# Three pieces of work moved inside the first units of a four-layer graph network: scaled values, the table of empty rows, and the softplus of two constants

## The chip, the cores and the metric

The kernel runs on one core of a Trainium2 chip. A core has a matrix engine (TensorE, PE in the profile; its weight loads are PEld), a vector engine (VectorE, DVE), an engine for activation functions (ScalarE, ACT), a general engine (GpSimd, POOL) and SyncE (SP), which here only issues DMA transfers. Each engine takes its own instructions strictly in the order of the program, and engines wait for each other through semaphores. The metric is the device time of one execution in microseconds; the kernel before took 1411.94 us, the median of three runs from 1405.89 to 1412.65.

## The reference

A batch of 8 graphs shares one adjacency matrix of 2048 x 2048 nodes; each node has 64 features. There are four layers, each with a residual and a layer norm around it. Layers 0, 1 and 2 are attention layers, layer 3 is a gated mean over neighbours. Cut to what matters:

```
# layer 0 (layers 1 and 2 alike, without the node weights and the inner norm)
h  = layernorm((x * node_weights + node_bias + x) @ W) * gamma + beta
s1, s2 = h @ a1, h @ a2
e  = leaky_relu(s1[:, :, None] + s2[:, None, :], 0.2)
att = softmax(where(adj > 0, e, -9e15), axis=-1)
x  = layernorm(x + elu(att @ h + h))
# layer 3
feat   = softplus(x * (w0 / sqrt(2)) + b0)
scores = feat * wa + ba
attn   = softmax over the neighbours j of scores[j, d], for each feature d
x  = layernorm(x + sum_j attn[i, j, d] * feat[j, d])
```

A row of the adjacency without any neighbour gets a softmax over equal numbers, which is the plain mean over all nodes. The kernel needs three small things for this: a table of the empty rows, the mean of the values, and, for layer 3, a bound on the scores, which it takes from the softplus of the two largest inputs that are possible.

## The kernel before, in words

A *unit* is one layer of one graph. Its 2048 x 2048 weights are made and used in 16 tiles of 128 neighbours by 2048 rows. For tile `jb` the vector engine makes `w` with one instruction (maximum of a row term and a per-neighbour term, times the mask: `weights`, line 981), and the matrix engine multiplies it in eight matmuls of 512 columns onto two PSUM banks `acc` (`products`, line 1030). The left operand of these matmuls is `pv`, the values scaled by an exponential of their score (`prepare`, line 811). There are four buffers for `w`, so VectorE can be up to four tiles ahead. The list `todo` orders the units: layer 0 of graphs 0 to 3, layer 1 of the same, layer 0 and 1 of graphs 4 to 7, and then layer 2 of all, with layer 3 beside and behind it. The first unit is number 0, the fourth is number 3, both in layer 0.

Everything else of a unit (its features, its scores, the norm behind it) is written as Python generators, which a `Streams` object (line 1358) steps once per tile. A generator yields where it wants to wait for a number of steps. All PE, DVE, ACT and POOL instructions are kept in the order in which the Python code issues them (`InOrder`, line 70), so this stepping decides what stands behind what in each engine's queue; no scheduler changes it later. What is waited for in one instruction holds everything behind it on the same engine.

The first unit is special in four ways.

- Its features are made by `features0(0)` (line 665) before any product. Its last part makes the normalised values `y` on ACT, completes them on POOL (`settle`), adds the 16 blocks of `y` in a *tree* of four POOL additions (8, 4, 2 and 1 blocks), and multiplies the sum by ones on PE (`p_mean`); then `mean_pieces` (line 613) splits the mean into three bf16 pieces, with ACT and DVE in turn. After the tree the loop that drives the start breaks off (`ready(0, 0)`), and `prepare(0, 0)` (line 1410) issues `pv` on POOL. In the queues the first tile's products are followed on PE by `p_mean`, and the fifth `w` on DVE stands behind the first piece of the mean.
- Its mask is still being made. `mask` (line 280) compares the adjacency rows with zero on DVE (`edge`, two instructions each) and counts neighbours on PE (`p_deg`, 16 tiny matmuls). Nine masks are made before the unit and seven during tiles 0 to 6, one ahead of each tile's `w`.
- After the last mask, `empties` (line 328) reads the counts on DVE (`empty`, `half_ldeg`), spreads them out (`em`), transposes them on PE (`p_empty`, four matmuls), and copies the result on DVE (`emptyT`). `emptyT` is read by the last matmuls of every unit; `half_ldeg` and `empty` are read only in layers 2 and 3.
- Its row term lies in SBUF; from unit 1 on the row term `r` is made by PE in PSUM ahead of the last products of the unit before (`spread`, line 827), with `Banks.use("psR", 1)` taking over the PSUM banks that `p_deg` and `p_empty` used.

`constants` (line 433) starts at tile 3 of the first unit. It makes the right operands `rh` of the three layers and the score operands, on POOL, PE and ACT, and then the bound for layer 3: `softplus` of `ext` (line 381: Abs, Exp, then Ln and Relu on ACT, then one addition `fext` on DVE), two products and a shift on POOL (`l3off`, `l3b`) with a maximum on DVE between them, and six small DVE instructions (`beyond`, `fext`). `beyond` is next used by `group(0)` before layer 2, `l3off` by layer 3. Ln lies in another table of activation functions than Exp, so ACT loads a table ahead of Ln and again ahead of the next Exp.

The features of the next units also run beside unit 0. `features0(1)` and `features0(2)` scale `x` on ACT (`xs`, one buffer), transpose it on PE (`p_xT`), copy it on ACT (`xT`) and multiply it on PE (`p_h`). Between `p_xT` and `xT` of graph 2, ACT's queue holds the 16 `xs` activations of graph 3 and eight `y` activations of graph 1.

Of the kernel before, what the change touches and what calls it, by code (L numbers as in the profile page):

```python
# [18 lines left out]
P = 128  # L19
# [31 lines left out]
def gnn4_kernel(ctx: ExitStack, tc: tile.TileContext, t, out):  # L51
# [326 lines left out]
    nc.gpsimd.memset(ext[:, 1:2], -X_MAX)  # L378
    fext = consts.tile([P, 2], F32, name="fext")

    def softplus(f, y, src):

        act.activation(y, src, AF.Abs, scale=l3c[:, 0:1], bias=l3c[:, 1:2])
        act.activation(y, y, AF.Exp, scale=-1.0)
        yield 1
        act.activation(y, y, AF.Ln, bias=1.0)
        act.activation(f, src, AF.Relu, scale=l3c[:, 0:1], bias=l3c[:, 1:2])
        yield 1
        dve.tensor_tensor(f, f, y, ALU.add)

    rs_w, last_w, a_cols = [], [], [None]
# [41 lines left out]
    def constants():  # L433

        for layer in range(3):
            rs, last = rs_w[layer], last_w[layer]
            rr = early.tile([P, F1], F32, tag="rr", name=f"rr_{layer}", bufs=2)
            pool.memset(rr, 0.0)
            pool.tensor_tensor(rr[:, :F], rs[:, :F], last, ALU.subtract)
            if layer == 0:  # L440
                pool.tensor_tensor(rr[:, :F], rr[:, :F], gamma, ALU.mult)
                for h in range(2):
                    pool.tensor_scalar(
                        rr[h * F : h * F + 1, :F], beta[h * F : h * F + 1], 2.0, None, ALU.mult
                    )
            for h in range(2):
                pool.memset(rr[h * F : h * F + 1, F:], 1.0)
            rh = consts.tile([P, 2, F1], F32, name=f"rh_{layer}")
            pool.memset(rh, 0.0)
            yield 1  # L450
            for h in range(2):
                sl = slice(h * F, (h + 1) * F)
                pool.tensor_copy(rh[sl, h, :], rr[sl])
            RH.append(rh)
            if layer == 0:
                AS.append(None)
                continue
            yield from pm_slots.take()
            p = psum(f"p_rt_{layer}")
            pe.transpose(p[:F, :P], rr[:, :F], ident)  # L460
            yield 1
            rt = early.tile([F, P], F32, tag="rt", name=f"rt_{layer}", bufs=1)
            act.copy(rt, p[:F, :P])
            pm_slots.give()
            yield from pm_slots.take()
            p = psum(f"p_as_{layer}")
            pe.matmul(p[:, :2], lhsT=rt, rhs=a_cols[layer], start=True, stop=True)
            as_ = consts.tile([P, 2, 2], F32, name=f"as_{layer}")
            pool.memset(as_, 0.0)
            yield 1  # L470
            for h in range(2):
                sl = slice(h * F, (h + 1) * F)
                act.copy(as_[sl, h, :], p[sl, :2])
            pm_slots.give()
            AS.append(as_)
        pool.tensor_tensor(ident2, ident[:, :F], ident[:, F:], ALU.add)
        pool.tensor_scalar(l3c[:, 0:1], l3c[:, 0:1], INV_SQRT2, None, ALU.mult)
        yield 1
        yield from softplus(fext, small.tile([P, 2], F32, tag="sp", name="sp_ext", bufs=1), ext)
        l3b = small.tile([P, F], F32, tag="l3b", name="l3b", bufs=1)  # L480
        pool.tensor_tensor(l3off, wa, fext[:, 0:1].to_broadcast([P, F]), ALU.mult)
        pool.tensor_tensor(l3b, wa, fext[:, 1:2].to_broadcast([P, F]), ALU.mult)
        dve.tensor_tensor(l3off, l3off, l3b, ALU.max)
        pool.tensor_scalar(l3off, l3off, -1.0, HEADROOM, ALU.mult, ALU.add)
        yield 1
        dve.tensor_reduce(beyond, wa, AX.X, ALU.max, apply_absolute_value=True)
        dve.tensor_tensor(fext[:, 0:1], fext[:, 0:1], fext[:, 1:2], ALU.subtract)
        dve.tensor_tensor(beyond, beyond, fext[:, 0:1], ALU.mult)
        dve.tensor_scalar(fext[:, 1:2], beyond, -1.0, None, ALU.mult)
        dve.tensor_tensor(beyond, beyond, fext[:, 1:2], ALU.max)  # L490
        dve.tensor_scalar(beyond, beyond, -L3_SPAN, None, ALU.add)
# [173 lines left out]
    def features0(b):  # L665

        n = f"0_{b}"
        step = K2 if b < NB else 4
        x = x_cur[b].v
        xs = early.tile([P, K, F], F32, tag="xs", name=f"xs_{b}", bufs=1)  # L670
        for k in range(K):
            act.activation(
                xs[:, k],
                x[:, k],
                AF.Identity,
                scale=nodes[:, k : k + 1],
                bias=nodes[:, K + k : K + k + 1],
            )
            if k % step == step - 1:
                yield 1  # L680
        yield from h_slots.take()
        yield from xT_slots.take()
        xT = tmp.tile([P, K2, P], F32, tag="xT", name=f"xT_{b}")
        sums = small.tile([P, 2], F32, tag="sums", name=f"sums_{b}", bufs=4)
        yield from transposed(xT, sums, xs, n)
        h = tmp.tile([P, K, F2], F32, tag="h", name=f"h_{b}")
        g0 = 0
        while g0 < 4:
            width = Banks.width()
            ps = []  # L690
            yield from pm_slots.take(width)
            for g in range(g0, min(g0 + width, 4)):
                p = psum(f"p_h_{b}_{g}")
                for k in range(2):
                    pe.matmul(
                        p[:, k * 2 * F2 : (k + 1) * 2 * F2],
                        lhsT=xT[:, 2 * g + k],
                        rhs=w0c.rearrange("p h f -> p (h f)"),
                        start=True,
                        stop=True,  # L700
                    )
                ps.append((g, p))
            yield 1
            for g, p in ps:
                act.copy(
                    h[:, 4 * g : 4 * g + 4, :], p[:, : 4 * F2].rearrange("p (k f) -> p k f", f=F2)
                )
            pm_slots.give(width)
            g0 += width
        xT_slots.give()  # L710
        yield from sq_slots.take()
        sq = tmp.tile([P, K, F], F32, tag="sq", name=f"sq_h_{b}")
        act.activation(sq, h[:, :, :F], AF.Square)
        yield 2
        st = small.tile([P, 2, K], F32, tag="st", name=f"st_h_{b}", bufs=4)
        if b < 2:
            dve.tensor_reduce(st[:, 1], sq, AX.X, ALU.add)
            sq_slots.give()
            yield from inv_std(st, K, f"h_{b}", centered=True)
        else:  # L720
            yield from side_stats(sq, f"h_{b}", st)
        rs = st[:, 1]
        sc = S[0, b] = Scores()
        s = small.tile([P, 2, K], F32, tag="s0", name=f"s_{n}")
        dve.tensor_tensor(
            s, h[:, :, F:].rearrange("p k w -> p w k"), bc_k(rs, 2, K), ALU.mult
        )
        dve.tensor_tensor(s, s, bc_f(s_off, 2, K), ALU.add)
        exponentials(sc, s[:, 0], s[:, 1], s, 0, b, n)()

        if in_psum(0, b):
            yield from pm_slots.take()
            p = psum(f"p_r_{n}")
            pe.transpose(p[:K, :P], sc.e[:, 0], ident)
            yield 1
            rows_term(sc, p[:K, :P], n, 0, b)
            pm_slots.give()
        else:
            first_row(sc)
        y = rows_tile(early, "y", f"y_{b}")  # L740
        for k in range(K):
            act.activation(y.block(k), h[:, k, :F], AF.Copy, scale=rs[:, k : k + 1])
            if k % step == step - 1 and k < K - 1:
                yield 1
        h_slots.give()
        y.settle()
        V[0, b] = y
        yield from e_slots.take()
        tree = tmp.tile([P, K2, F], F32, tag="e", name=f"tree_{b}")
        src = y.v  # L750
        for m in (8, 4, 2, 1):
            pool.tensor_tensor(tree[:, :m], src[:, :m], src[:, m : 2 * m], ALU.add)
            src = tree
        yield 3
        yield from pm_slots.take()
        p = psum(f"p_mean_{n}")
        pe.matmul(p[:, :F], lhsT=ones, rhs=tree[:, 0], start=True, stop=True)
        e_slots.give()
        yield 1
        yield from mean_pieces(sc, p[:, :F], n)  # L760
# [639 lines left out]
    for i, _ in enumerate(first):  # L1400
# [6 lines left out]
            bg.step()  # L1407
        if ready(0, 0):
            break
    prepare(0, 0)  # L1410
    prepared.add(0)
    for layer in range(3):
        load_constants(layer)
# [22 lines left out]
    for n, (layer, b) in enumerate(todo):  # L1436
# [10 lines left out]
        for jb in range(K):  # L1447
            if n == 0:
                while masks < min(K, 9 + jb):
                    mask(p_deg, masks)  # L1450
                    masks += 1
                    if masks == K:
                        empties(p_deg)
            now[2] = jb
            reach(K * n + jb)
            u = units[n]
# [540 lines left out]
```

## Time and profile before

| what | value |
|---|---|
| median of three runs | 1411.94 us |
| profiled execution | 1418.37 us, its span 1416.6 us |
| busy: PE, DVE, ACT, POOL | 87%, 85%, 58%, 54% of the span |
| chain that ended last | PE 51%, DVE 21%, ACT 12%, POOL 8% |
| first product of unit 0 | 60.02 us |
| first product of unit 1 | 125.25 us |
| PE busy in 90 to 120 us | 21.14 of 30 us |
| PE busy in 150 to 180 us | 28.61 of 30 us |
| mean granted clock of TensorE | 0.94 |

Nearly every instruction has line 80 in the profile (the helper that keeps the order), so instructions are told apart by the tile that they write. `acc` is a product, `w` a weight tile, `edge` a mask. One tile's products are eight matmuls; they take 1.87 to 1.94 us at full clock and 3.68 us at half clock. In a list in order of time, the brackets at the end of a line give the idle time of the engine ahead of it and what ended it.

### The profile page before, as it was taken

Reading aid. Unit: us, or ns where it says so; the run is one execution under the profiler, and the core shown is the slowest. Engines: PE = TensorE matmul, PEld = TensorE weight load, DVE = VectorE, ACT = ScalarE, POOL = GpSimd, SP = SyncE. Lnnn points to the kernel's source line nnn. Section 1 sums busy time; section 2 is a strip of 40 time slices with the busy share of each in tenths; the row PEclk is TensorE's granted clock in tenths of the full one; section 3 lists DMA queues with packets and bytes.
Section 4 is the critical chain, followed back from the end, with each engine's and each line's share of the span. In section 5 each row is a group of like instructions: output and inputs, shape, how many; then the busy total and the mean of one; then the engine's idle time right before and its main releaser. Section 6 shows DMA issues by size and latency. Waiting matters only on the chain.

```text
span 1416.6 us, 19533 instructions
## 1 busy us (share of the span) xinstructions
PE 1232.4 (87%) x7169; PEld 628.2 (44%) x7169; DVE 1208.4 (85%) x1108; ACT 821.6 (58%) x1593; POOL 758.5 (54%) x1075
## 2 busy tenths in 40 slices
PE   3587989899898997999999878789989899976996
PEld 3233323334343332343333323245654555666996
DVE  3777989999998999989999788998879798977876
ACT  3434544565666553556546997877576767664442
POOL 1435776556765674554553432534455565666665
PEclk9698989999999998999999897999999999998998
DMA  8640000000000121222101000025543434511111
GB/s 293 210 103 1 2 1 2 1 2 1 3 2 0 48 88 45 91 91 62 61 2 39 1 15 1 22 60 144 140 138 85 135 105 134 159 40 34 35 38 33
DMA packets 112010, 87.24 MB, mean 62 GB/s; under 512 B 57917, under 2 KB 90845, under 8 KB 110882
## 3 DMA queue, kind: packets, MB, share of 16 engines
q1 hardware_dynamic: 111538, 85.79, 20.8%
q8 instruction: 59, 0.97, 0.3%
q14 instruction: 45, 0.37, 0.1%
q10 hardware_dynamic: 368, 0.12, 0.0%
HBM read 60.40 MB, written 25.45 MB: 61 GB/s over the span
## 4 chain that ended last, share of the span: by engine, by line
PE 51%; DVE 21%; ACT 12%; POOL 8%; issue 6%; DMA 2%; SPq 0%; DVEq 0%; POOLq 0%; ACTq 0%
PE acc L80 28%; PE p_l L80 14%; DVE w L80 13%; ACT w L80 2%; PE p_o L80 2%; ACT x L80 2%; DVE o L80 2%; PE r L80 2%; PE p_s L80 2%; POOL sq_x L80 1%; POOL tree L80 1%; ACT y L80 1%; ACT xs L80 1%; POOL st_x L80 1%; DMA raw<-in_adjT_dram 1%
## 5 line engine op out<-in xcount | busy, mean ns | idle before, releaser
L80 DVE SCALAR_TENSOR_TENSOR w<-r,se,edge 128x2048 f32<-128x2048 f32 (+1 forms) x270 | 552.9, 2101 | 29.2 <-PE r L80 22.9
L80 PE MATMUL acc<-w,pv 128*64 128x512 f32 x2048 | 501.3, 624 | 59.7 <-DVE w L80 38.6
L80 DVE SCALAR_TENSOR_TENSOR w<-r,lo_g,edge 128x2048 f32<-128x2048 f32 (+1 forms) x144 | 297.8, 2097 | 26.8 <-PE acc L80 14.6
L80 ACT ACTIVATE w<-w,down_g 128x2048 f32<-128x2048 f32 (+1 forms) x144 | 256.9, 1809 | 64.4 <-DVE w L80 57.3
L80 PEld LDWEIGHTS p_l<-v,mask 128*128 128x128 f32 x2048 | 256.3, 196 | 61.8 <-issue 48.5
L80 PE MATMUL acc<-w,x 128*64 128x512 f32 x1024 | 265.2, 648 | 17.6 <-ACT w L80 14.9
L80 PE MATMUL p_l<-v,mask 128*128 128x256 f32 x2048 | 271.1, 291 | 10.6 <-POOL mask L80 7.0
L80 PEld LDWEIGHTS acc<-w,pv 128*64 128x64 f32 x2048 | 134.7, 140 | 318.1 <-issue 190.7
L80 POOL TENSOR_TENSOR sq_x<-sq_x 128x32 f32<-128x32 f32 (+4 forms) x207 | 110.1, 532 | 63.8 <-ACT sq_x L80 49.4
L80 PEld LDWEIGHTS acc<-w,x 128*64 128x64 f32 x1024 | 67.4, 144 | 139.3 <-issue 88.9
L80 ACT ACTIVATE x<-o,st_x 128x64 f32<-128x64 f32 x256 | 91.6, 445 | 12.2 <-POOL st_x L80 12.2
L80 ACT ACTIVATE nd<-p_l,empty 128x256 f32<-128x256 f32 x64 | 30.2, 471 | 109.3 <-PE p_l L80 109.3
L80 ACT ACTIVATE o<-p_o,den 128x64 f32<-128x64 f32 x256 | 55.8, 323 | 45.9 <-DVE den L80 45.9
L80 PE MATMUL p_o<-rh,oT 128*128 128x130 f32 x384 | 61.6, 297 | 23.4 <-DVE o L80 6.7
L80 ACT COPY oT<-acc 128x512 f32<-128x512 f32 x48 | 25.7, 587 | 89.4 <-PE acc L80 89.4
L80 PEld LDWEIGHTS p_o<-rh,oT 128*128 128x128 f32 x384 | 50.1, 197 | 57.7 <-issue 33.7
L80 POOL TENSOR_TENSOR st_x<-isw_x,mhalf 128x16 f32<-128x16 f32 x24 | 70.5, 2938 | 1.9
L80 POOL TENSOR_TENSOR eh<-eh,x 128x1024 f32<-128x1024 f32 (+2 forms) x24 | 36.4, 1530 | 44.8 <-ACT eh L80 44.8
L80 DVE RECIPROCAL nd<-nd 128x256 f32<-128x256 f32 x32 | 55.7, 1742 | 0.0
L80 POOL TENSOR_TENSOR d<-x,wa_bc 128x1024 f32<-128x1024 f32 x8 | 19.0, 2380 | 66.7 <-DVE x L80 66.7
L80 POOL CAST rT<-rT 16x128 bf16<-16x128 f32 x45 | 15.2, 339 | 66.4 <-ACT rT L80 62.9
L80 POOL TENSOR_TENSOR sq_x<-o 128x512 f32<-128x512 f32 x23 | 29.2, 1270 | 34.6 <-DVE o L80 34.1
(258 smaller groups left out, 1543.8 us busy)
## 6 DMA issues: line engine op xcount, KB each, us to landing
mask<-mask_d SPq DMA_DIRECT2D x132, 256.0 KB
mask_d<-mf SPq DMA_DIRECT2D x32, 512.0 KB
raw<-in_adjT_dram SPq DMA_DIRECT2D x8, 1024.0 KB
raw<-in_adjT_dram SPq DMA_DIRECT2D x16, 512.0 KB
x<-in_x_dram SPq DMA_DIRECT2D x8, 512.0 KB
x_d<-x SPq DMA_DIRECT2D x8, 512.0 KB
e<-x_d SPq DMA_DIRECT2D x64, 64.0 KB
out_dram<-o SPq DMA_DIRECT2D x64, 64.0 KB
```

The source lines that it names most:

```text
L80: ins = f(*args, **kwargs)
```

## The change

Three things move; no instruction is added or taken away on any engine, and SP's queue has the same order as before.

- `prepare(0, 0)` is called inside `features0(0)` ahead of the tree, so `pv` of unit 0 stands ahead of the four tree additions in POOL's queue.
- `empties` is issued at tile 13 of unit 0, where before it was issued behind the last mask, ahead of tile 7's `w`. On DVE its four instructions now stand behind the tile 12 `w` and ahead of the tile 13 `w`; on PE the four `p_empty` matmuls stand behind the products of tile 12.
- `constants` waits until unit 3 has begun before the softplus of `ext`, and this softplus leaves four steps, not one, between its Relu on ACT and its addition on DVE. In the queues: the ACT instructions now stand around the scores of layer 1, graph 0; the DVE addition `fext` and `l3off` behind tile 5's `w` of unit 3; the six small DVE instructions behind tile 6's `w`; the three POOL instructions behind the splitting of `rT`. ACT still loads tables twice for it, the second time ahead of the Exp of unit 2's `eh`.

```diff
-    def softplus(f, y, src):
+    def softplus(f, y, src, layer=2):
 
         act.activation(y, src, AF.Abs, scale=l3c[:, 0:1], bias=l3c[:, 1:2])
         act.activation(y, y, AF.Exp, scale=-1.0)
         yield 1
         act.activation(y, y, AF.Ln, bias=1.0)
         act.activation(f, src, AF.Relu, scale=l3c[:, 0:1], bias=l3c[:, 1:2])
-        yield 1
+        yield 1 if layer == 2 else 4
         dve.tensor_tensor(f, f, y, ALU.add)
...
         pool.tensor_scalar(l3c[:, 0:1], l3c[:, 0:1], INV_SQRT2, None, ALU.mult)
-        yield 1
-        yield from softplus(fext, small.tile([P, 2], F32, tag="sp", name="sp_ext", bufs=1), ext)
+        while now[1] < 3:
+            yield 1
+        yield from softplus(fext, small.tile([P, 2], F32, tag="sp", name="sp_ext", bufs=1), ext, 0)
         l3b = small.tile([P, F], F32, tag="l3b", name="l3b", bufs=1)
...
         y.settle()
         V[0, b] = y
+        if b == 0:
+            prepare(0, 0)
         yield from e_slots.take()
         tree = tmp.tile([P, K2, F], F32, tag="e", name=f"tree_{b}")
...
         if ready(0, 0):
             break
-    prepare(0, 0)
     prepared.add(0)
...
                 while masks < min(K, 9 + jb):
                     mask(p_deg, masks)
                     masks += 1
-                    if masks == K:
-                        empties(p_deg)
+                if jb == K - 3:
+                    empties(p_deg)
```

## The prediction

> **What bounds the kernel now.** I read the page's shares first, then the chain that ended last in order of time, then DVE, PE, POOL and ACT in order of time from 45 to 130 us. Over the whole span PE (87%) and DVE (85%) are both nearly full, so a change at the start is worth what it takes from the start: later units repeat the same queues and hand a shift on. The start is not full, and the chain shows why. From the chain, start and length in us:
>
> ```profile
> 47.49 4.27 POOL tree L80
> ...
> 56.03 3.95 POOL pv L80
> 60.02 3.68 PE acc L80 x8
> 63.71 0.62 PE p_mean L80 x2
> ...
> 110.29 1.28 ACT L80
> ```
>
> The reader sees three places that the change touches: `pv` behind the tree, PE starting when `pv` ends, and the table load ahead of Ln in the middle of unit 0. DVE in order of time gives the stalls with their releasers:
>
> ```profile
> 64.90 0.29 DVE L80 SCALAR_TENSOR_TENSOR mean<-mean,later,mean 128x64 f32<-128x64 bf16 x1 [6.68 <-ACT mean L80]
> 83.23 0.18 DVE L80 TENSOR_SCALAR empty<-p_deg 128x16 f32<-128x16 f32 x1 [3.56 <-PE p_deg L80]
> 84.61 0.69 DVE L80 CAST emptyT<-p_empty 128x512 bf16<-128x512 f32 x1 [0.75 <-PE p_empty L80]
> 85.22 6.87 DVE L80 SCALAR_TENSOR_TENSOR w<-row,se,edge 128x2048 f32<-128x2048 f32 x3
> 112.10 0.16 DVE L80 TENSOR_TENSOR fext<-fext,sp_ext 128x2 f32<-128x2 f32 x1 [10.20 <-ACT fext L80]
> 113.06 2.34 DVE L80 SCALAR_TENSOR_TENSOR w<-row,se,edge 128x2048 f32<-128x2048 f32 x1
> 115.64 2.19 DVE L80 TENSOR_TENSOR beyond<-beyond,fext 128x1 f32<-128x1 f32 x1
> ```
>
> PE in order of time shows what these cost it, and that it comes back slowly after a gap:
>
> ```profile
> 83.92 0.66 PE L80 MATMUL p_empty<-ident,em 128*128 128x128 f32 x4 [0.73 <-DVE em L80]
> 87.62 6.29 PE L80 MATMUL acc<-w,pv 128*64 128x512 f32 x16 [3.04 <-DVE w L80]
> 109.75 1.90 PE L80 MATMUL p_h<-w0c,xT 128*128 128x132 f32 x8 [5.04 <-ACT xT L80]
> 115.46 3.68 PE L80 MATMUL acc<-w,pv 128*64 128x512 f32 x8 [3.82 <-DVE w L80]
> 119.08 1.88 PE L80 MATMUL r<-row,ones 3*128 3x512 bf16 x4
> 120.89 3.30 PE L80 MATMUL acc<-w,pv 128*64 128x512 f32 x8
> ```
>
> One tile is 3.68 us at half clock and 1.94 at full clock. The stretches of 2 us show the granted clock at 1.00 in 84 to 86 us, 0.53 in 86 to 88, 0.50 to 92 and 0.76 in 92 to 94: the 3.04 us gap closed it, and it opened some 5.4 us after work came back (93.0 less 87.62). After 60.02 it took 9.5 us, after 115.46 8.2 us.
>
> **Part one, `pv` ahead of the tree.** POOL and DVE take turns here: `tree` of 512 columns takes 4.26 us at 47.49 but 1.26 at 106.37, where DVE is idle, and `pv` takes 3.94 here and 1.90 at 109.33. `pv` begun at 47.49 gets its turn when the DVE work of 47.08 to 50.5 is over, so it ends near 52.4 (49.3 to 50.5, plus 1.9). That frees PE 7.6 us earlier for one tile only: the next PE instruction is `p_mean`, and it now waits for the tree. What is late next is therefore the tree, not `pv`. POOL's five instructions are the same and their turns lie between the same DVE instructions, so I put the tree's end at 60.0, about where `pv` ended (59.97); bounds are 58.1, if all additions slip in between masks, as the third and fourth did, and 63.1, if POOL gets no turn until DVE's fourth `w` ends at 58.2 (1.9 + 2.8 + gaps). `p_mean` was at 63.63, so it comes 3.6 us earlier. DVE's stall of 6.68 shrinks by the same. Behind `p_mean`, PE needed 19.56 us up to the last count (83.19), with the clock opening 5.9 us in. PE now has a gap before `p_mean`, so it opens 5.4 to 9.5 us in; between nothing and 1.8 us are lost, I take 0.7. The last count ends at 60.0 + 19.56 + 0.7 = 80.3: part one is worth 2.9 us (from -1.3, with the tree at 63.1 and the full clock loss, to 5.5). The reloads of the adjacency issued by masks 12 and 13 shift along: they are released by DVE, and 2 MB landed between 57 and 64 us at 258 to 420 GB/s, so they stay hidden. The constants' small POOL instructions (60 to 64.5 us) lose DVE's idle time as cover. About ten of them may have to wait a turn; they have until `st_h` at 78.75, 14.23 us of idle POOL, so I cost them at nothing. No moved step issues a transfer, and SP's queue keeps its order.
>
> **Part two, the empty rows' table at tile 13, with part three's removal of the softplus from unit 0.** Call the end of the last count T (83.19 before, 80.3 after).
>
> - At tile 7 DVE no longer waits for the counts (3.56) and the transposes (0.75). It goes on from the last mask, which ended 3.5 us ahead of T, so tile 7's `w` is ready at T - 1.2, and PE goes on at full clock. Before, PE idled 0.73 + 3.04 us and then ran two tiles in 6.29 instead of 3.8.
> - Tiles 7 to 11 with `p_rt`, `p_r`, `p_as` and `p_xT` took 13.5 us (87.62 to 101.13), 11.0 at full clock. DVE's `w` at 2.3 us each with 0.6 for `s` reach tile 11 at T + 8.6, PE wants it at T + 8.2. So `p_xT` ends near T + 11.8. POOL's `st_h` (3.08 us, begun at 78.75) is no longer beside an idle DVE; if it holds tile 7's `w` back until its end that is 2.1 us, if not, nothing. DVE's masks ran at their usual 1.31 beside it, so I take nothing and keep 2.1 for the range.
> - Tile 12 ends at T + 13.7, `p_empty` (0.66) at T + 14.4, `emptyT` 0.7 later, then `w` of tile 13 (2.34): its products start at T + 17.4. The gap of 3.0 us is the same as at tile 7, and again closes the clock: 3.68, to T + 21.1.
> - The next PE work is `p_h`, which waits for ACT's `xT`. That took 8.6 us from the end of `p_xT` (101.13 to 109.75), of which 0.5 was the softplus' first two activations; so it is ready at T + 19.9. Before, this wait stood open as 5.04 us; now it lies under the gap and the slow tile. The moved bubble is thus mostly free.
> - `p_h` 1.9 at half clock to T + 23.0; tile 14's `w` has long been ready, as DVE's wait of 10.20 for `fext`, 0.66 for `l3b` and the 3.0 us of the six small instructions are gone. The clock opens 5.4 to 8.2 us after T + 17.4, so tile 14 takes 2.6 and `r` ends 1.0 later, at T + 26.6.
> - Before, `r` ended at 120.89 = T + 37.7. The two are worth 11.1 us at `r`, from 8.2 (`st_h` holds DVE and the clock stays shut) to 12.6. PE's own first product of unit 1 gains a little more, but unit 1 is paced by DVE, whose nine `w` from 141.29 on follow each other without a gap, and DVE starts behind `r`. POOL's `tree` and `pv` of unit 1 ran on an idle DVE (106.37 to 111.2); now they lie beside the last `w`. Even if they wait for DVE's last `w` at about T + 22, 5 us more end before the first product of unit 1 at T + 29.7.
>
> **Part three, what unit 3 pays.** On ACT, the Abs, Exp, table load, Ln and Relu fall into the idle stretch 214.0 to 216.3 us (ACT waits 2.32 us for `p_r` at 216.31), some 8 us ahead of DVE's addition at about 224, so DVE doesn't wait for ACT. DVE pays 0.16 + 0.66 + 0.22 us for `fext`, the wait for POOL and `l3off`, then 0.8 us for six instructions, and up to 2 us more if POOL's addition to `o` (2.38 at 226.09) blocks one of them as it did `mean` there (2.10 at 226.45); that block is paid already today. I take 2.0. This stretch is DVE's on the chain (`w` 219.62 to 237.65), so it counts in full. PE's wait of 1.67 us at 229.2 becomes about 3.2, at the border of closing the clock; closed, it costs up to 2.3 us more. I take half of it, in all 3.0 lost (bounds 1.0 and 5.0). The second table load, 1.28 us ahead of an Exp at 229.82, delays POOL's `eh` and `pv` of a unit that starts at 255, 20 us later: nothing.
>
> **Sum.** 2.9 + 11.1 - 3.0 = 11.0 us less. The profiled execution (1418.37, of which 1.8 lie outside its span) becomes 1407.4; it stands 6.4 above the median, so the median becomes 1400.9.
>
> **The rivals.**
>
> - *The clock stays open in the moved gap.* It needs the 3.0 us gap at tile 13 and the 3.2 us one in unit 3 to end before the gate falls; 84 to 88 us speaks against it, the open clock behind the 1.67 us gap at 230.87 a little for it. Tile 13 then takes 1.94 and ends at T + 19.3, `p_h` begins at T + 19.9 and takes 1.1, tile 14 and `r` end at T + 23.9: 2.7 more, and 1.0 in unit 3, in all 14.7 less, 1397.2. The Trainium skill's "TensorE: Matmul & The Clock Gate", section "What's actually happening", states this: the gate goes by free-running windows of about 3.4 us, so a shorter gap need not close it. By that rule both outcomes are open from one run to the next; the trace's 3.04 us gap closed it.
> - *Part one does nothing, because `p_mean` takes over from `pv`.* If the tree ends at 63.1, 11.1 - 3.0 = 8.1 less or a little under, 1403.8. For it speaks that PE's order has `p_mean` second; against it that the third and fourth addition slipped in between masks.
> - *Half of the gain is lost on the way:* `st_h` holds DVE, the clock stays shut long in units 0 and 3, the tree is late. 0.5 + 8.2 - 5.0 = 3.7 less, 1408.2, no measurable change.
> - *The stall moves along (slower).* If ACT gives `fext` in unit 3 as late as in unit 0, DVE waits 10.20 us there, with a shut clock afterwards (1.75 for each of two tiles) and 3.0 for the rest: 16.7 lost against 14.0 won, 1414.6. It decides from a wait of about 7.5 us, that is with `fext` later than 231 us on the old axis. Against it: the four steps left, and ACT's queue, which is empty at 214.
>
> **How the numbers follow.** The forecast has 0.50, the open clock 0.08, part one at nothing 0.12, half the gain 0.18, the moved stall 0.07, and 0.05 stays for shifts in later units that I can't see. Half a per cent, 7.1 us, is about what a measurement can tell from no change. Faster takes the first two and most of the third, 0.68; same the rest of the third, the fourth and half of the fifth, 0.24; slower 0.08. The range leaves out the far end of the open clock and the moved stall: 1395 to 1410. The likeliest case alone is 1397 to 1405.
>
> **What would show it.** In the new profile: `pv` on POOL ends by 53 and one tile's products stand alone on PE, followed by a gap that `p_mean` ends at about 60; no DVE wait at tile 7, and tile 7's products without a gap ahead of them; a gap of about 3 us on PE ahead of tile 13, with half clock behind it; no wait of DVE for ACT's `fext` anywhere; unit 1's first product at 109 to 111 us instead of 125.25; in unit 3 DVE about 2 us later at tile 7. The forecast is wrong if the first product of unit 1 comes after 116, if DVE waits for `fext` in unit 3, or if the lead at unit 1 (15 us) is not found at the start of layer 2.

## The result, and the profile after

The changed kernel took 1394.89 us (median of five runs from 1394.77 to 1401.63), beside 1411.94 for the kernel before (five runs from 1405.89 to 1414.3). The ratio is 0.9899, 95% interval 0.9866 to 0.9931, that is 14.3 us less, between 9.7 and 18.9. The profiled execution took 1401.63 us with a span of 1399.8, 16.8 less than the span before. Shares of busy time: PE 1220.0 us (87%), DVE 1208.8 (86%), ACT 821.6 (59%), POOL 770.2 (55%); mean granted clock 0.951. The work is the same, it lies closer together.

PE of the changed kernel in order of time, which answers to the PE lines of before (start, length, what, and in brackets the idle time ahead and what ended it):

```profile
52.22 3.37 PE L80 MATMUL acc<-w,pv 128*64 128x512 f32 x8 [6.50 <-POOL pv L80]
59.81 0.69 PE L80 MATMUL p_mean<-tree,ones 128*128 128x64 f32 x2 [4.22 <-POOL tree L80]
...
79.27 0.18 PE L80 MATMUL p_deg<-zeros_h,edge 128*128 128x32 bf16 x1
79.38 3.65 PE L80 MATMUL acc<-w,pv 128*64 128x512 f32 x16
...
92.75 0.66 PE L80 MATMUL p_empty<-ident,em 128*128 128x128 f32 x4
96.44 3.45 PE L80 MATMUL acc<-w,pv 128*64 128x512 f32 x8 [3.04 <-DVE w L80]
99.82 1.17 PE L80 MATMUL p_h<-w0c,xT 128*128 128x132 f32 x8
100.92 1.94 PE L80 MATMUL acc<-w,pv 128*64 128x512 f32 x8
102.79 1.03 PE L80 MATMUL r<-row,ones 3*128 3x512 bf16 x4
...
106.75 1.94 PE L80 MATMUL acc<-w,pv 128*64 128x512 f32 x8 [0.35 <-issue]
```

The three parts can be read off. One tile stands alone at 52.22, and `p_mean` then waits for the tree. Tile 7's products follow the last count (79.27) without a gap. The gap of 3.04 us is now ahead of tile 13, and `p_h`, which used to wait 5.04 us for ACT, follows without a wait. The last line is the first product of unit 1: 106.75 instead of 125.25, 18.5 us earlier.

DVE of the same kernel in order of time, first in unit 0, then in unit 3:

```profile
61.08 0.28 DVE L80 SCALAR_TENSOR_TENSOR mean<-mean,later,mean 128x64 f32<-128x64 bf16 x1 [1.50 <-ACT mean L80]
61.79 0.69 DVE L80 TENSOR_SCALAR edge<-raw 128x1024 fp8e4<-128x1024 int32 x1 [0.43 <-DMA raw<-in_adjT_dram]
63.05 0.70 DVE L80 TENSOR_SCALAR edge<-raw 128x1024 fp8e4<-128x1024 int32 x1 [0.56 <-DMA raw<-in_adjT_dram]
...
93.44 0.69 DVE L80 CAST emptyT<-p_empty 128x512 bf16<-128x512 f32 x1 [2.65 <-PE p_empty L80]
...
200.80 4.60 DVE L80 SCALAR_TENSOR_TENSOR w<-r,se,edge 128x2048 f32<-128x2048 f32 x2
205.32 0.14 DVE L80 TENSOR_TENSOR fext<-fext,sp_ext 128x2 f32<-128x2 f32 x1
206.12 0.23 DVE L80 TENSOR_TENSOR l3off<-l3off,l3b 128x64 f32<-128x64 f32 x1 [0.66 <-POOL l3b L80]
...
208.82 1.85 DVE L80 TENSOR_TENSOR fext<-fext 128x1 f32<-128x1 f32 x1
...
211.55 20.54 DVE L80 SCALAR_TENSOR_TENSOR w<-r,se,edge 128x2048 f32<-128x2048 f32 x10
```

The wait of 6.68 us for the mean has become 1.50, and two short waits for reloaded adjacency rows have appeared behind it. The waits for the counts (3.56) and for `fext` (10.20) are gone; what the softplus costs DVE in unit 3 is its instructions, a wait of 0.66 us for POOL, and 1.85 us for an addition of one column, which ends with POOL's addition to `o` beside it (208.31 to 210.66).

The lead of the changed kernel over the kernel before, taken at the matmuls with `emptyT` that close each unit's products, is 18.5 us at the end of unit 0, 17.9 and 19.1 at units 1 and 2, 16.9 at unit 3, 16.6 to 17.0 through the next twelve units, and 17.3 for the last eight. So in this pair of profiles the change is made in unit 0, a little of it is paid in unit 3, and the units behind hand the lead on within 0.7 us. Run 8 below shows that this steadiness does not hold in every pair.

### The profile page after: what moved, and what is told of

Same layout as the page of the kernel before. It is cut to its first block, busy times and chain, and to the rows that moved or that the text cites. A ratio compares the mean times of both kernels' runs of the same rounds, so it can differ in the third digit from the quotient of the medians.

```text
span 1399.8 us, 19531 instructions
## 1 busy us (share of the span) xinstructions
PE 1220.0 (87%) x7169; PEld 624.2 (45%) x7169; DVE 1208.8 (86%) x1108; ACT 821.6 (59%) x1593; POOL 770.2 (55%) x1075
## 4 chain that ended last, share of the span: by engine, by line
PE 49%; DVE 24%; ACT 11%; issue 7%; POOL 6%; DMA 2%; SPq 1%; ACTq 0%; DVEq 0%; POOLq 0%
PE acc L80 26%; DVE w L80 16%; PE p_l L80 14%; ACT w L80 2%; PE p_o L80 2%; ACT x L80 2%; DVE o L80 1%; PE r L80 1%; PE p_s L80 1%; POOL sq_x L80 1%; DMA raw<-in_adjT_dram 1%; DVE nd L80 1%; POOL st_x L80 1%; DVE edge L80 1%; ACT y L80 1%
## 5 line engine op out<-in xcount | busy, mean ns | idle before, releaser
L80 PE MATMUL acc<-w,pv 128*64 128x512 f32 x2048 | 494.1, 615 | 53.0 <-DVE w L80 39.4
L80 PE MATMUL acc<-w,x 128*64 128x512 f32 x1024 | 261.8, 640 | 19.2 <-ACT w L80 16.3
L80 ACT ACTIVATE x<-o,st_x 128x64 f32<-128x64 f32 x256 | 91.5, 445 | 13.2 <-POOL st_x L80 13.2
L80 PE MATMUL p_o<-rh,oT 128*128 128x130 f32 x384 | 61.9, 298 | 24.4 <-DVE o L80 6.7
L80 PEld LDWEIGHTS p_o<-rh,oT 128*128 128x128 f32 x384 | 50.2, 197 | 58.3 <-issue 32.3
L80 ACT ACTIVATE xs<-x,nodes 128x64 f32<-128x64 f32 x128 | 44.7, 434 | 3.2 <-PE p_xT L80 3.2
```

Source lines behind the costliest of these rows:

```text
L80: ins = f(*args, **kwargs)
```

## The experiments

Runs 1 to 4 shared runs of the kernel before with a median of 1411.74 us (1408.5 to 1413.44); runs 5 to 8 shared others with 1417.7 (1406.6 to 1420.15); runs 9 and 10 others with 1412.61 (1409.66 to 1419.95). A difference in us below is the distance of the ratio from 1, times that median. T is the end of the last count of neighbours in unit 0, as in the prediction.

### One part alone

**Run 1: the kernel before, with `pv` ahead of the tree.**

```diff
+        if b == 0:
+            prepare(0, 0)
...
-    prepare(0, 0)
     prepared.add(0)
```

> Only the scaled values of unit 0 are made ahead of the tree; the empty rows' table and the softplus stay where they were. My theory: the mean's matmul takes over from the scaled values, because it stands second in PE's queue, so PE's first product comes near 52 us, stands alone, and the mean's matmul ends the gap at 59.8 us. The last count ends near 79.4 us (83.2 before), the first product of unit 1 comes near 121.5 us (125.25 before), and the kernel is 3.8 us faster (2.5 to 5). Rival one, the scaled values alone were on the path: first product of unit 1 at 117.5 us, 7.6 us faster. Rival two, the later stall on the softplus swallows it: unit 1 at 125 us, no change.

Measured: 1408.33 us, ratio 0.9982 (0.9969 to 0.9994), 2.5 us less (0.8 to 4.4). PE of this run in order of time:

```profile
59.51 0.69 PE L80 MATMUL p_mean<-tree,ones 128*128 128x64 f32 x2 [4.17 <-POOL tree L80]
...
121.34 1.94 PE L80 MATMUL acc<-w,pv 128*64 128x512 f32 x8 [0.35 <-issue]
```

`pv` no longer holds PE (the first product is at 51.91), and the tree holds it instead. Unit 1's first product is 3.9 us earlier, not the 8.1 by which unit 0's first product moved. That `p_mean` takes over all of the gain, or none of it, is out.

**Run 2: the kernel before, with the empty rows' table at tile 13.**

```diff
-                    if masks == K:
-                        empties(p_deg)
+                if jb == K - 3:
+                    empties(p_deg)
```

> Only the empty rows' table is made in tile 13. My theory: tiles 7 to 12 come 6 us earlier, but DVE then still waits for the softplus on ACT, which hangs on the transposes of graph 2 (11.0 us from the end of those transposes to DVE's addition, as before). The transposes end near 94.7 us (101.13 before), DVE's addition comes near 105.7 us (112.10), the products of tile 14 near 109 us (115.46): 6.4 us faster (4 to 8). Rival, a bubble of 3 us is only moved from tile 7 to tile 13: products of tile 14 at 115 us, no change. Rival, the table's move carries the whole gain: 13 us faster or more.

Measured: 1405.58 us, ratio 0.9954 (0.9937 to 0.9971), 6.5 us less (4.1 to 8.9). The same view of this run, with DVE's addition `fext` behind it:

```profile
98.90 3.68 PE L80 MATMUL acc<-w,pv 128*64 128x512 f32 x8 [3.04 <-DVE w L80]
...
107.74 3.23 PE L80 MATMUL acc<-w,pv 128*64 128x512 f32 x8 [3.10 <-DVE w L80]
```

```profile
104.38 0.16 DVE L80 TENSOR_TENSOR fext<-fext,sp_ext 128x2 f32<-128x2 f32 x1 [5.53 <-ACT fext L80]
```

With the stall at tile 7 gone and the gap ahead of tile 13 free, the softplus is what is late next: DVE now waits 5.53 us for `fext`, and PE waits 3.10 us behind that for tile 14, which starts at T + 25.8 (before T + 32.3). Unit 1 starts 8.0 us earlier relative to T.

**Run 3: the kernel before, with the softplus in unit 3.**

```diff
-        yield 1
+        yield 1 if layer == 2 else 4
         dve.tensor_tensor(f, f, y, ALU.add)
...
-        yield 1
+        while now[1] < 3:
+            yield 1
```

> Only the softplus of the constants is left to unit 3. My theory: DVE's wait of 10.2 us goes, but PE still waits for ACT's copy of the transposes until 109.2 us, so the products of tile 14 come at about 111.2 us instead of 115.46 and the row term of unit 1 ends 5 us earlier; unit 3 pays 1.8 us. 3.5 us faster in all (2 to 6). Rival, the stall counted in full: 10 us faster. Rival, the stall moves to unit 3: no change, with a DVE wait for the softplus there.

Measured: 1410.27 us, ratio 0.9975 (0.9959 to 0.9990), 3.5 us less (1.4 to 5.8) by the ratio, while the medians alone differ by 1.5. PE of this run:

```profile
108.59 1.66 PE L80 MATMUL p_h<-w0c,xT 128*128 128x132 f32 x8 [4.53 <-ACT xT L80]
110.18 3.21 PE L80 MATMUL acc<-w,pv 128*64 128x512 f32 x8
```

The wait of `p_h` for ACT stays, so all but 0.5 of its 5.04 us was not the softplus; what goes is the second wait, ahead of tile 14. Unit 1 starts 7.3 us earlier relative to T, and unit 3 takes some 2 of them back.

**Run 4: the changed kernel without part one** (`prepare` behind the tree again, the diff of run 1 undone).

> The changed kernel without its first part: the scaled values stand behind the tree again. My theory: everything after the last count is as in the changed kernel, 3.8 us later: last count at 83.2 us, first product of unit 1 near 110.6 us (106.75 in the changed kernel), 13.2 us faster than before (11 to 15). That is more than the two parts alone give together (6.4 and 3.5), because each alone leaves the other's wait standing at tile 14. Rival, the parts add up: 10 us faster.

Measured: 1400.76 us, ratio 0.9922 (0.9905 to 0.9939), 11.0 us less (8.6 to 13.4). I had expected 13.2. Unit 1's first product is at T + 27.22; in the changed kernel it is at T + 27.30 (and at T + 28.55 in run 8, the same kernel once more). So part one does nothing behind T that these profiles can tell. The two parts alone gave 6.5 and 3.5, together 10.0; that they help each other, which I had expected to show here, is not seen: the times add up within their intervals, and relative to T unit 1 starts 8.0 and 7.3 us earlier in runs 2 and 3 and 14.8 in run 4. Runs 1 and 4 together (2.5 + 11.0 = 13.5) agree with the 14.3 of the whole change.

### The moved gap

Three runs, with the changed kernel once more beside them.

**Run 5: the changed kernel, `emptyT` copied by ACT.** This takes the gap ahead of tile 13 away, as DVE no longer waits for the transposes.

```diff
-        dve.tensor_copy(emptyT, q)
+        act.copy(emptyT, q)
```

> The changed kernel, with the last copy of the empty rows' table on ACT instead of DVE, so that DVE's weight of tile 13 no longer waits for PE and the gap of 3.04 us on PE ahead of tile 13 goes. My theory: the gap costs next to nothing in the changed kernel, because the features' matmuls behind tile 13 wait for ACT's copy of the transposes until 98.9 us whatever DVE does. PE's idle time moves behind tile 13 (about 3.6 us, ended by ACT) and the row term of unit 1 ends between 0.9 us earlier and 2.3 us later than in the changed kernel (later if the clock closes in the new gap): no change against it, 1.0% faster than the kernel before. Rival, the gap is on the path: 3 us faster than the changed kernel.

**Run 6: the changed kernel, graph 3's features started three tiles later.** This takes 16 `xs` activations out of ACT's queue ahead of `xT`.

```diff
-    begin = {(0, 1): 2, (0, 10): 3, (4, 4): 4, (5, 4): 5, (6, 4): 6, (8, 4): 7}
+    begin = {(0, 1): 2, (0, 13): 3, (4, 4): 4, (5, 4): 5, (6, 4): 6, (8, 4): 7}
```

> The changed kernel, with the features of graph 3 begun at tile 13 of unit 0 instead of tile 10, so that ACT copies graph 2's transposes ahead of the 16 scaling activations of graph 3. My theory: ACT's copy is ready some 6 us earlier, but PE reaches the features' matmuls only at 99.8 us, behind the gap and the slow tile 13: no change against the changed kernel (within 1 us at the first product of unit 1, 106.75 us). Rival, the features' wait was what held unit 0: 3 us faster or more.

**Run 7: runs 5 and 6 together.**

> The changed kernel with both: the table's copy on ACT and graph 3's features begun at tile 13. My theory: the gap on PE and the wait for ACT lie beside each other in the changed kernel, each covering the other, so only both together gain: products of tile 13 follow tile 12 and the transposes without a gap at full clock, row term of unit 1 ends near 99.5 us, its first product comes near 102.4 us instead of 106.75, and the kernel is 4 us faster than the changed one (2 to 5). Rival, the two gain what they gain alone: no change against the changed kernel. Rival, unit 1 then waits for something else (the scaled values of graph 1 on POOL): less than 1 us.

**Run 8: the changed kernel, unaltered.**

> The changed kernel once more, beside the three others, as their yardstick: 1.0% faster than the kernel before (0.7% to 1.3%), first product of unit 1 near 106.5 us. If the theory that the whole gain is made in unit 0 is right, the first weight of each later unit comes 16 to 18 us earlier than before, up to the end.

| run | median us | ratio (95%) | unit 1 starts at |
|---|---|---|---|
| 5, table by ACT | 1399.33 | 0.9894 (0.9851 to 0.9937) | T + 30.29 |
| 6, graph 3 later | 1397.45 | 0.9864 (0.9819 to 0.9908) | T + 29.42 |
| 7, both | 1393.07 | 0.9850 (0.9817 to 0.9882) | T + 24.52 |
| 8, changed kernel | 1397.85 | 0.9881 (0.9844 to 0.9919) | T + 28.55 |

PE of run 5:

```profile
93.26 1.94 PE L80 MATMUL acc<-w,pv 128*64 128x512 f32 x8
98.93 2.13 PE L80 MATMUL p_h<-w0c,xT 128*128 128x132 f32 x8 [3.73 <-ACT xT L80]
100.99 3.68 PE L80 MATMUL acc<-w,pv 128*64 128x512 f32 x8
```

PE of run 6:

```profile
97.83 3.68 PE L80 MATMUL acc<-w,pv 128*64 128x512 f32 x8 [3.45 <-DVE w L80]
101.44 2.05 PE L80 MATMUL p_h<-w0c,xT 128*128 128x132 f32 x8
```

PE of run 7:

```profile
92.65 1.94 PE L80 MATMUL acc<-w,pv 128*64 128x512 f32 x8
94.52 1.17 PE L80 MATMUL p_h<-w0c,xT 128*128 128x132 f32 x8
...
102.70 1.94 PE L80 MATMUL acc<-w,pv 128*64 128x512 f32 x8 [1.43 <-POOL pv L80]
```

Without the gap ahead of tile 13, run 5 has a gap of 3.73 us right behind it, for `xT`, and is no faster. Run 6 has `xT` early and keeps the gap (3.45 us), and is no faster either. Relative to T, both are later than I had expected: in run 5 the row term `r` ends 3.0 us later than in the changed kernel (at most 2.3 expected), and in run 6 unit 1 starts 2.1 us later than there (within 1 expected), or 0.9 later than in run 8. Only when both causes go does the stretch close up: unit 1 starts 2.8 us earlier relative to T than in the changed kernel and 4.0 earlier than in run 8. The two waits lay on top of each other, and taking away one shows the other. Run 7's median is 4.8 us under that of run 8, but their intervals overlap, so that it beats the changed kernel is likely and not shown. The next wait in it is `pv` of unit 1 on POOL, 1.43 us.

Run 8 missed its own expectation, a lead over the kernel before of 16 to 18 us in every unit. Taken at the same matmuls as above, its lead is 19.6 us at the end of unit 0, of which 2.2 are an earlier start of the whole execution, then 15.1 in units 4 to 7, 13.8 at unit 16 and 21.7 at the end, where the changed kernel had 17.3. So not all of the time between two single profiles is made in unit 0. In the last eight attention units TensorE spent 37 us at half clock in run 8, 51 in the changed kernel and 62 in the kernel before; that this is what moves the lead there was not tested.

### What is left of part one

**Run 9: the changed kernel, with graph 0's mean two steps later.** It removes the wait of `p_mean` by giving the tree two more tiles.

```diff
-    bg.all.append([first, 0])
+    bg.all.append([first, 2])
```

> The changed kernel, with the rest of the first features' generator (the mean's matmul and its pieces) taken up two tiles later, so that the mean no longer stands between the products of tiles 0 and 1. The streams that share its slots shift a little with it. My theory: PE's gap of 4.2 us ahead of the mean's matmul goes, but only PE moves up; DVE, which paces unit 0 from tile 8 on, had waited only 1.5 us for the mean, and its next mask then waits for the adjacency rows until 61.8 us anyway. Last count up to 3 us earlier, row term of unit 1 within 1.5 us of the changed kernel: no change against it (1.0% faster than the kernel before). Rival, the mean's wait is on the path: 3 us or more faster than the changed kernel.

Measured: 1402.42 us, ratio 0.9912 (0.9880 to 0.9945), no better than the changed kernel's 0.9899. DVE of this run:

```profile
61.65 0.77 DVE L80 TENSOR_SCALAR edge<-raw 128x1024 fp8e4<-128x1024 int32 x1 [2.84 <-DMA raw<-in_adjT_dram]
```

and PE:

```profile
64.99 0.43 PE L80 MATMUL p_mean<-tree,ones 128*128 128x64 f32 x2
...
74.20 3.51 PE L80 MATMUL acc<-w,pv 128*64 128x512 f32 x8 [1.91 <-DVE w L80]
...
99.12 3.68 PE L80 MATMUL acc<-w,pv 128*64 128x512 f32 x8 [4.56 <-DVE w L80]
```

`p_mean` no longer waits (it follows its neighbours at 64.99), but now the reloaded adjacency rows do not arrive in time, DVE loses 2.84 us to them, PE idles 1.91 us at 74.20, and T comes 27.2 us behind the first product of unit 0, as in the changed kernel. (T itself, 78.6, is 0.8 earlier, but POOL's completion of `y`, ahead of everything that was changed, is 0.8 earlier too.) So the gap of 4.2 us ahead of `p_mean` was worth nothing up to T. Behind T other background work has moved too (graph 1's mean now stands ahead of tile 14) and the row term of unit 1 ends 4.5 us later, where I had expected it within 1.5. This run therefore tells only the first half cleanly: behind the tree stands the transfer.

**Run 10: run 7 with the same two steps.**

> The kernel with the table's copy on ACT and graph 3's features begun at tile 13, and with the mean taken up two tiles later as well. By the same theory no gain over the kernel without the last step (1.5% faster than the kernel before, within 0.3%); if the mean is on the path once the two other waits are gone, 3 us more (1.7%).

Measured: 1402.44 us, ratio 0.9912 (0.9886 to 0.9937), against 0.9850 (0.9817 to 0.9882) for run 7, which was measured beside other runs of the kernel before: worse, by intervals that just miss each other, where I had expected no difference. PE of this run:

```profile
100.59 0.69 PE L80 MATMUL p_mean<-tree,ones 128*128 128x64 f32 x2 [3.83 <-POOL tree L80]
```

This is the mean of graph 1, which the shift has brought ahead of tile 14 in PE's queue, while its tree on POOL is not done. The gap that run 7 had closed is open again for another reason.

### The clock, from the traces at hand

The trace notes the granted clock with the times of its changes. In each of the twelve profiles (before, after and the ten runs) these changes lie a whole multiple of 3.413 us apart, on a grid with a phase of its own in every profile. Cut along this grid, the windows show what goes ahead of each change. Columns: stretch, its length, busy time of PE, PEld, DVE, ACT and POOL with the number of instructions, granted clock, DMA share and rate. The kernel before, around the gap ahead of tile 7:

```profile
82.72:86.13 3.41, 1.12 (x21) 0.78 (x19) 2.15 (x5) 0.31 (x2) 0.68 (x4) 1.00 1.00 213
86.13:89.54 3.41, 1.92 (x6) 0.69 (x8) 3.41 (x2) 0.00 (x0) 0.00 (x0) 0.50 0.00 0
89.54:92.96 3.42, 3.42 (x12) 0.95 (x10) 3.35 (x6) 0.43 (x3) 0.00 (x0) 0.50 0.00 0
92.96:96.37 3.41, 3.41 (x18) 0.97 (x14) 3.41 (x2) 0.38 (x2) 0.00 (x0) 1.00 0.00 0
```

The changed kernel, around the gap ahead of tile 13 and then in unit 3:

```profile
92.70:96.12 3.42, 0.70 (x6) 0.42 (x4) 2.68 (x2) 3.42 (x14) 0.40 (x1) 1.00 0.04 9
96.12:99.53 3.41, 3.09 (x8) 0.77 (x8) 3.41 (x3) 3.40 (x11) 3.27 (x3) 0.50 0.00 0
99.53:102.94 3.41, 3.41 (x19) 1.57 (x18) 2.40 (x1) 0.81 (x3) 3.25 (x3) 1.00 0.02 5
...
208.76:212.17 3.41, 1.94 (x8) 0.48 (x8) 3.27 (x9) 1.27 (x5) 2.17 (x3) 1.00 0.00 0
212.17:215.59 3.42, 1.64 (x8) 0.48 (x8) 3.42 (x2) 3.39 (x4) 0.27 (x1) 1.00 0.01 2
```

Run 8, which is the same kernel, in unit 3:

```profile
212.40:215.82 3.42, 0.64 (x4) 0.34 (x6) 3.38 (x5) 2.90 (x4) 0.00 (x0) 1.00 0.00 0
215.82:219.23 3.41, 3.41 (x12) 0.90 (x8) 3.41 (x2) 1.59 (x2) 2.69 (x2) 0.50 0.01 2
219.23:222.64 3.41, 3.41 (x18) 1.12 (x16) 3.41 (x3) 0.00 (x0) 3.41 (x2) 1.00 0.02 5
```

In these windows the busy share of PE in the window that has just ended tells what comes next. Before, the gap takes up the end of one window and reaches 1.5 us into the next: the first (1.12 of 3.41) shuts the clock, the second (1.92 of 3.41) is not busy enough to open it again, and it stays shut for two windows. After, a gap of the same 3.04 us ends 0.3 us behind the edge, the next window is full enough (3.09), and it stays shut for one. In unit 3 the gap of 3.18 us is cut in two by an edge, both halves are about half busy, and the clock doesn't shut at all; in run 8 the grid lies 0.2 us later and the gap 1.2 us later, so that it falls almost wholly into one window, and the clock shuts.

I counted this over the windows of the first four units (44 to 236 us) in all twelve. Of windows at full clock, all 39 with PE busy under 0.40 of the time were followed by half clock, 25 of the 26 between 0.43 and 0.57 by full clock, and of the 36 from 0.58 to 0.80 33 by full clock. Of windows at half clock, 70 of the 71 under 0.80 were followed by half clock again, and of the 72 above it 59 by full. The border is not sharp: from 44 to 1380 us, of 85 windows at full clock with PE busy 0.40 to 0.50, 35 were followed by full clock. Nor is the busy share all that counts. In the first four units six windows of twelve profiles were fully busy at full clock and still followed by half clock. All six hold the ten small matmuls `p_s` (4 and 64 columns) and the four of `r` (3 rows) that end some units, about 2.3 of the 3.41 us; over the whole programs all 17 windows at full clock that hold these matmuls whole were followed by half clock. So it seems that such matmuls count for less than the busy time that the view gives them. All this is a reading of counts; no run set the phase on purpose or varied the matmuls.

## Why the prediction was right, and where its terms were off

The forecast of the likeliest case was right in its direction and in the places where most of the time was to be won, lost or waited for. The ratio puts the time at 1397.7 beside the median of 1411.94, inside both ranges; the median itself, 1394.89, lies 0.1 under the low end. The sum was too small, 11.0 against 14.3 (9.7 to 18.9) by the ratio and 16.8 in the profiled span. The two gains were sized too small and the cost too large. Unit 1's first product came at 106.75, ahead of the 109 to 111 that were to show it.

| term | predicted | in the profiles |
|---|---|---|
| part one: T earlier | 2.9 | 83.19 - 79.45 = 3.7, of which 0.2 is an earlier start |
| parts two and three at `r`: its end behind T | 37.7 - 26.6 = 11.1 | 37.8 - 24.4 = 13.4 |
| from `r` to unit 1 | a little | 18.5 - 17.1 = 1.4 |
| unit 3 pays | 3.0 | 18.5 - 16.9 = 1.6 |
| in all | 11.0 | 16.9 |

The prediction took 120.89 us for the end of `r` before, which is where the next row starts; `r` ends at 119.08 + 1.88 = 120.96, T + 37.8.

- **Part one.** `pv` ended at 52.2 (predicted 52.4), one tile stood alone, and `p_mean` started at 59.81 (predicted 60.0). "What is late next is therefore the tree" held. The loss of 0.7 us for a late clock did not come: from `p_mean`'s start PE needed 19.64 us to T, against 19.56 before. DVE's stall of 6.68 us shrank by 5.2 and not by the same 3.6, because DVE's own work ahead of it ended later: its fourth `w` at 59.6 instead of 58.2, as the third took 3.99 us instead of 3.35 and the mask behind it 2.88 instead of 2.07. The step that failed without harm is "so they stay hidden", of the adjacency's reloads: they came onto DVE's path with 0.43 and 0.56 us, as the mean's wait had covered them. PE did not wait for DVE up to T; run 9 shows the wait of 2.84 us that comes up once the mean no longer stands ahead of the masks.
- **Tile 7 to tile 13.** No wait at tile 7 and full clock behind it, `p_xT` ended at T + 11.5 (predicted 11.8), tile 13 started at T + 17.0 (17.4) after a gap of 3.04 us (3.0). The fear that `st_h` holds `w` back was not borne out.
- **"The moved bubble is thus mostly free"** held, and runs 5 to 7 show it: taking the bubble away alone gains nothing, because the wait for `xT` stands behind it. The other half, that the softplus accounts for 0.5 us of `xT`'s lateness and not more, is run 3's 4.53 us.
- **The mis-sized term is the clock behind tile 13.** I wrote that the clock opens 5.4 to 8.2 us after work comes back. It opened 3.1 us after (96.44 to 99.53). Tile 13 took 3.45 instead of 3.68, `p_h` 1.17 instead of 1.9, tile 14 1.94 instead of 2.6: with the 0.4 of the start that is 2.0 of the 2.2 us missing at `r`. The clock was also the 1.4 us gained behind `r`: before, the gap ahead of tile 14 left half clock up to tile 15 (3.30 us), after it took 1.94. I had read 5.4, 8.2 and 9.5 us (the trace notes the change at 69.06, so the last is 9.0) as a delay counted from the work's return. In these traces it is a count of whole windows, and where the work returns in a window is chance: the same gap in run 2 left 6.8 us of half clock (98.00 to 104.82), in run 8 3.4 (96.34 to 99.76).
- **Unit 3.** DVE has 8.94 us between the fifth and the eighth `w` before and 10.75 after, so it pays 1.8 of the predicted 2.0. PE's gap became 3.18 us (predicted 3.2, at the border). Of the up to 2.3 us for the clock none was paid. The step's error is deeper than its odds: in run 8 the clock did shut there, and yet the eighth `w` of unit 3 and the first of the next unit lie 22.77 us apart (235.55 - 212.78) against 22.70 in the changed kernel (234.25 - 211.55). So DVE sets the pace in that stretch: at full clock PE waits 0.32 us for each `w` there, and it makes up for the slow window out of these waits.
- **The rivals.** The open clock (1397.2) came nearest in time, but only half for its reason: in unit 3 the clock stayed open, in the moved gap it shut as forecast and opened sooner. The Trainium skill's "TensorE: Matmul & The Clock Gate", section "What's actually happening", gives the gate free-running windows of 3413 ns; the grid of 3.413 us in all twelve traces agrees. The same section of the Trainium skill has the clock fall after at least one idle window; the measurement differs and decides here, as windows with PE busy up to 0.39 of the time were enough. Part one at nothing is refuted by run 1. Half the gain and the moved stall did not happen: DVE waits for ACT's `fext` nowhere.

The lead of 15 us that was to be found at the start of layer 2 was 16.6 to 17.

## What to carry to other kernels

At the start of a kernel, before its queues are full, a stall is a stack of waits: take one away and ask of each engine what is late next, and price the edit by the distance to that. A wait that can't be removed is best put where another engine is late anyway, and two waits that lie over each other have to go together or not at all. A lead won at the start is kept to the end only where the later stages repeat the same queues, so read it at every stage, not only at the end, and in more than one profile: the same changed kernel ended its attention layers 17.3 and 21.7 us ahead of the same profile of before.

## What the runs showed of the hardware that I had not expected

- **The granted clock changes on a fixed grid of 3.413 us, whose phase differs from profile to profile.** A gap of about 3 us cost PE nothing, one window of half clock or two, by where an edge cut it: 0 in unit 3 of the changed kernel, 3.41 us in unit 0, 6.83 us in unit 0 of the kernel before. At half speed a full window loses half its work, 1.7 us, so an edit that leaves a gap of this size can be sized only to about 3 us from one trace.
- **The start moves by itself.** POOL's completion of `y` in unit 0, ahead of anything that was changed, starts between 43.41 us (run 8) and 45.85 (run 6); 45.62 before, 45.41 after. Differences of 2 us between two single profiles at the start are therefore no evidence. Times relative to T are steadier, but the clock moves them too: the changed kernel had unit 1 at T + 27.30 once and at T + 28.55 in run 8.
- **POOL and DVE held each other up where both worked from SBUF.** In unit 0, where the row term lies in SBUF, `pv` took 4.90 us on POOL and DVE's `w` beside it 3.99 instead of 2.34. In unit 1, where the row term lies in PSUM, `pv` took 1.90 beside `w`. In unit 3 a DVE addition of one column out of SBUF took 1.85 us and ended with POOL's addition. That the place of the operands decides is a reading of these rows; it wasn't tried. In the changed kernel, first in unit 0 and then in unit 1:

```profile
47.27 4.90 POOL L80 TENSOR_TENSOR pv<-y,se 128x1024 f32<-128x1024 f32 x1
50.33 3.99 DVE L80 SCALAR_TENSOR_TENSOR w<-row,se,edge 128x2048 f32<-128x2048 f32 x1
...
103.41 1.90 POOL L80 TENSOR_TENSOR pv<-y,se 128x1024 f32<-128x1024 f32 x1
103.92 6.99 DVE L80 SCALAR_TENSOR_TENSOR w<-r,se,edge 128x1024 f32<-128x1024 f32 x4 [1.99 <-issue]
```
